# One block of exact products per batch: four projections moved behind a blockwise convolution

## The chip, the cores and the metric

The kernel runs on one core of a Trainium2 chip. The metric is device time in microseconds from one launch, the median over runs. Beside the runs there is one profiled execution, whose trace all views of the profile come from.

## What is computed

The input is `x` (32 batches of 512 rows by 512 columns, float32) and one 0/1 adjacency matrix of 512 by 512. Two layers follow each other:

```
# layer 0: attention over the graph, 8 heads of 64 columns, residual, layer norm
q, k, v = x @ Wq + bq, x @ Wk + bk, x @ Wv + bv
scores = einsum('bihd,bjhd->bhij', q, k) / 8 + where(adj == 0, -1e9, 0)
x = layernorm(x + einsum('bhij,bjhd->bihd', softmax(scores), v))
# layer 1: graph convolution, residual, layer norm
x = layernorm(x + (adj @ x) @ weight + bias)
```

## The kernel before, in words

**Exact products.** A product that must keep float32 accuracy is made of three passes on TensorE, each of four matmuls of 128x128 by 128x512. `split_high`, `split_rest` and `split_both` (L303 to L310) turn an operand into three factors, HIGH (by ACT), REST (by DVE) and BOTH (by POOL); the weights have such factors too. HIGH and REST passes add up in one PSUM bank, called near, the BOTH pass in another, called far. Everything that reads near and far adds them (`finish_projection`, L431, with ACT and DVE; `add_near` and `add_far`, L562 and L566, with DVE). The factors of the current left operand lie in three tiles of 128 x 4 x 512 that `factors` (L327) hands out; they have one buffer each, so x of batch b+1, then y of batch b-1 (the aggregated rows), then x of batch b+2 take turns in it.

**PSUM.** All eight banks are one ring (`bank`, L200): a new bank is the one that was given out eight banks ago, and TensorE waits until that has been read.

**The order.** The order of all instructions is written out by hand in `iteration(b)` (L805); each engine, and the queue of SP that issues the DMAs, works off its own in that order. `run` (L728) emits a list of steps, `merge` (L795) puts the k-th list of other steps behind the k-th of a list. `AFTER` (L882) hands steps over to the next iteration. Iteration b does, on TensorE:

1. `attend(b, 0)` and `attend(b, 1)`: the exponentials of heads 0 to 3 times v (L632).
2. `scores(b, 1)`: keys times queries of heads 4 to 7 (L609). DVE adds the mask while it empties a bank (L611), ACT takes the exponential in place (L613), POOL adds the four tiles of a pair of heads up (`add_exponentials`, L624) and `fold_squares` (L654) transposes that sum on DVE and reduces it to the softmax's denominators. Both tiles of POOL's sums and the eight exponential tiles are rings as well.
3. The first four of the eight projections of batch b+1 (`project`, L438; weights stream in from DRAM in chunks, `fetch_chunk`, three ahead).
4. `attend(b, 2)`, `attend(b, 3)`, then `scores(b + 1, 0)`.
5. The last four projections, the four blocks of v of batch b+1 (`project_values`, L461), the aggregation of batch b-1 with the adjacency matrix (`aggregate`, L527) and its convolution with the second layer's weight (`convolve`, L572), one block of rows after the other (`FIRST_TWO` and `whole`).

Between these stand, for the other engines: `turn_out` (L636, DVE transposes the attention's output and SP writes it out), `fetch_rows` (L648, it comes back transposed), `scale_rows` and `add_rows` (L693 and L700, ACT and POOL), `pass_parts`, `fetch_parts` and `add_up` (L668, L673 and L680, the denominators), `statistics`, `square_root`, `invert_root` and `normalise` (L478 to L501, the layer norms), `load_squares` and `turn_squares` (L223 and L344, x of batch b+2), `add_bias` (L547) and `store` (L513). `square_root` and the exponential need different function tables in ACT, so ACT loads a table (ACT_TABLE_LOAD) at each change.

In the kernel before, x of batch b+2 is split into factors after the whole convolution of batch b-1; the first projections that read it come in the next iteration, after two attends and a score block.

Of the kernel before, what the change touches and what calls it, by code (L numbers as in the profile page):

```python
# [9 lines left out]
FR = mybir.dt.float32r  # L10
# [8 lines left out]
P = 128  # L19
# [159 lines left out]
HIGH, REST, BOTH = 0, 1, 2  # L179
# [3 lines left out]
def fast_kernel(ctx: ExitStack, tc, verdict, x, adj, Wq, bq, Wk, bk, Wv, bv, W1, b1, out):  # L183
    nc = tc.nc
    B, N, D = x.shape
    H = Wq.shape[1] // HD
    HP = H // 2
    NB = N // P
    DB = D // P
# [4 lines left out]
    work = ctx.enter_context(tc.tile_pool(name="work", bufs=2))  # L194
# [5 lines left out]
    def bank(*shape):  # L200

        return psum.tile([P, *shape], FP, name="bank", tag="bank", bufs=8)
# [85 lines left out]
    def load_adjacency_rows(c):  # L288
        IN["adj", c] = work.tile([P, N], FP, name="adj_rows", tag="turn", bufs=TURNS)
        nc.sync.dma_start(IN["adj", c], adj[c * P:(c + 1) * P, :])  # L290
# [30 lines left out]
    def shrunk(w):  # L321
# [2 lines left out]
        nc.scalar.activation(temp, w, AF.Copy, scale=SHRINK)  # L324
        return temp

    def factors():  # L327
        return [work.tile([P, DB, N], FR, name=f"factors{f}", bufs=1) for f in (HIGH, REST, BOTH)]

    def x_transpose(c):  # L330

# [30 lines left out]
    def turns(b):  # L362
        return [(turn_squares, b, d) for d in range(DB)] if b < B else []
# [57 lines left out]
    def one_pass(f, pm, left, right, blocks=range(DB)):  # L421

        for d in blocks:
            nc.tensor.matmul(pm, left(f, d), right(f, d), start=(f != REST and d == 0),  # L424
                             stop=(f != HIGH and d == DB - 1))
# [43 lines left out]
    def projections(b):  # L469

        return [(project, b, which, m) for which, m in SEQUENCE] if b < B else []
# [90 lines left out]
    def add_near(b, r, near):  # L562
        row = X[b][:, r, :]
        nc.vector.scalar_tensor_tensor(row, near, 1.0 + EPSILON, row, op0=ALU.mult, op1=ALU.add)  # L564

    def add_far(b, r, far):  # L566
        row = X[b][:, r, :]
        nc.vector.tensor_add(row, far, row)  # L568

    NEAR, FAR = {}, {}  # L570

    def convolve(b, passes):  # L572

        yt = YT[b]
        for r, f, blocks in passes:
            if (b, r) not in NEAR:
                NEAR[b, r], FAR[b, r] = bank(N), bank(N)
            one_pass(f, (FAR if f == BOTH else NEAR)[b, r], lambda f, d: yt[f][:, d, r * P:(r + 1) * P],
                     lambda f, d: w1[:, f, d, :], blocks)
# [17 lines left out]
    E, ES, OUT, AT, ROWS, PART, INVERSE, TURNED, PASSED = ({} for _ in range(9))  # L597
# [28 lines left out]
    def attend(b, hp):  # L626
        po = bank(N)
        for j in range(NB):
            e = E.pop((b, hp, j))
            for s in range(2):  # L630
                h = 2 * hp + s
                nc.tensor.matmul(po[s * HD:(s + 1) * HD, :], V[b, j][:, h * HD:(h + 1) * HD], e[:, s, :],  # L632
                                 start=(j == 0), stop=(j == NB - 1))
        OUT[b, hp] = po

    def turn_out(b, hp):  # L636

        po = OUT.pop((b, hp))
        at = AT[b, hp] = work.tile([P, N], FP, name="attT")
        if b == B - 1:  # L640
            nc.scalar.activation(at, po, AF.Copy)  # L641
            return

        nc.vector.transpose(at, po)  # L644
        TURNED[b, hp] = passing.tile([P, N], FP, name="turned")
        nc.sync.dma_start(TURNED[b, hp], at)
# [69 lines left out]
    seen = consts.tile([P, 3], FP, name="seen")  # L716
# [11 lines left out]
    def run(units):  # L728
        for unit in units:
            unit[0](*unit[1:])  # L730
# [42 lines left out]
    def norm(t, which):  # L773

        if t - which < 0:
            return []
        lo, hi = which * NB, (which + 1) * NB
        return [(square_root, t, slice(lo, hi)), (invert_root, t, slice(lo, hi))] + [
            (normalise, t, slot) for slot in range(lo, hi)]

    def folds(b, g):
        return [(fold_squares, b, hp) for hp in range(g * PAIRS, (g + 1) * PAIRS)]

    def survey(b, which=1):
# [20 lines left out]
    def iteration(b):  # L805

        units = projections(b + 1)
        scaled, added = residuals(b, 0)
        later_scaled, later_added = residuals(b, 1)
        turned, divided = turns(b + 2), splits_of_x(b + 2)  # L810
        splits, gathered = aggregation(b - 1)
        squares = [(load_squares, b + 2, d) for d in range(DB)]
        folded = folds(b, 1)

        attend(b, 0)
        turn_out(b, 0)
        sooner, later = AFTER.pop(b - 1, ([], []))
        run(sooner)
        attend(b, 1)
        turn_out(b, 1)  # L820
        if b > 0:
            fetch_parts(b, 0)
        take_scores(b, 1)
        run(later)
        waiting = [(fetch_rows, b, 0), (fetch_rows, b, 1)]
        looking = 2 <= b < 2 + NB
        look = [(look_for_low_half, b - 2)] if looking else []
        ready = 1 if looking else 0 if b < 2 else 2
        run(waiting[:ready])
        if b == 0:  # L830
            run(merge(units[:4], [waiting + [(fold_squares, b, 1), (pass_parts, b, 0), (fetch_parts, b, 0)], [],
                                  [(add_up, b, 0)],
                                  folded[:1]]))
        else:
            old, young = norm(b - 1, 1), norm(b - 1, 0)
            roots = slice(0, 2 * NB if b > 1 else NB)
            if b == 1:
                run(survey(0, 0))
            run(merge(units[:4], [waiting[ready:]
                                  + [(square_root, b - 1, roots), (add_up, b, 0), (invert_root, b - 1, roots)],  # L840
                                  folded[:1] + old[2:], [(store, b - 2)] if b > 1 else [], young[2:] + scaled]))
        attend(b, 2)
        turn_out(b, 2)
        load(b)
        if looking:
            load_adjacency_rows(b - 2)
        attend(b, 3)
        turn_out(b, 3)
        if b == 0:
            run(scaled)  # L850
        later = scores(b + 1, 0)
        run(added + later + folded[1:])

        run(merge(units[4:], [[(pass_parts, b, 1), (fetch_parts, b, 1)], look, [(fold_squares, b + 1, 0)], splits[:2]]))
        units = values(b + 1)
        chunks = [(fetch_chunk, (b + 2) * len(SEQUENCE) + n) for n in range(AHEAD)]
        squares += [(fetch_rows, b, 2), (fetch_rows, b, 3), (pass_parts, b + 1, 0)] + chunks
        run(merge(units, [[(add_up, b, 1)], [(fold_squares, b + 1, 1)] + squares, later_scaled if b == B - 2 else [],
                          turned[:1] + (later_added if b == B - 2 else [])]))
        if b == B - 2:  # L860
            load(B - 1)
        if b == 0:
            split_last_weight()
        run(merge(gathered, [[unit] for unit in turned[1:]]))
        fresh, seen, shift = survey(b, 0), survey(b - 1), biases(b - 1)
        high, rest, both = divided
        if b == 0:
            run(high + rest + both[::-1] + later_scaled + later_added)
            return
        convolve(b - 1, FIRST_TWO)  # L870
        if b == B - 2:
            run([(add_row, b - 1, 0), (add_row, b - 1, 1)] + shift[:2] + fresh + seen[:2])
            return
        run(later_scaled + later_added[:1] + [(add_row, b - 1, 0)] + shift[:1] + later_added[1:])
        run([(add_row, b - 1, 1)] + shift[1:2] + seen[:1])
        convolve(b - 1, whole(2))
        run([(add_row, b - 1, 2)] + shift[2:3] + fresh[:1])
        convolve(b - 1, whole(3))
        run(high + rest + [(add_row, b - 1, 3)] + shift[3:] + both)
        AFTER[b] = (fresh[1:] + seen[1:2], seen[2:])  # L880

    AFTER = {}  # L882

# [80 lines left out]
    high, rest, both = splits_of_x(1)  # L964
# [73 lines left out]
```

## Time and profile before

| what | us |
|---|---|
| median of 3 runs (lowest to highest) | 2567.88 (2567.47 to 2568.14) |
| the profiled execution's own time | 2570.15 |
| its span, from first to last instruction | 2568.3 |
| PE busy | 2558.8 |
| DVE busy | 2058.3 |
| POOL busy | 1751.8 |
| ACT busy | 1528.5 |

The granted TensorE clock is 0.999 over the span. PE is TensorE's matmuls, PEld its weight loads, DVE the vector engine, ACT the scalar engine, POOL GpSimd, SP the engine whose queue issues the DMAs. In the timeline a line begins with its start and its length in us, then the engine, the source line, the operation, the tiles (written <- read), the shapes and how many instructions are merged in it; brackets tell idle time of the engine just before and what ended it. In the groups a line has busy time and the mean ns of one, then the idle time. A matmul of the attention in float32 shows as two records.

### The profile page before, as it was taken

How to read it: one execution, taken by the hardware profiler on the slowest of the kernel's cores; microseconds unless marked ns; L12 is line 12 of the kernel's file. 1: busy time of each engine (PE TensorE's matmuls, PEld its weight loads, DVE VectorE, ACT ScalarE, POOL GpSimd, SP SyncE). 2: the span in 40 equal slices, each digit the busy share in tenths (PEclk: the TensorE clock that was granted, in tenths of full speed). 3: DMA queues.
4: the chain of work that ended last, by engine and by line, in shares of the span. 5: the costliest groups of instructions: out<-in, count | busy, mean ns of one | idle time of the engine just before them, and what ended most of it. 6: DMA issues, size and time to landing. Idle time of an engine off the chain costs nothing.

```text
span 2568.3 us, 36882 instructions
## 1 busy us (share of the span) xinstructions
PE 2558.8 (100%) x11324; PEld 1692.3 (66%) x11324; DVE 2058.3 (80%) x3796; ACT 1528.5 (60%) x2540; POOL 1751.8 (68%) x1104
## 2 busy tenths in 40 slices
PE   9999999999999999999999999999999999999998
PEld 6676666666676666766667676666766667666666
DVE  8878878788787887877888778877787787887878
ACT  5656655666555666556665565655657556565555
POOL 4776667666676666766767676676766766666767
PEclk9999999999999999999999999999999999999999
DMA  9655554554545645456455465554655546555441
GB/s 266 167 158 150 161 154 117 165 156 151 166 113 150 168 138 163 125 138 177 136 156 133 133 174 138 164 133 123 173 143 160 148 113 167 146 158 163 108 121 52
DMA packets 747291, 380.59 MB, mean 148 GB/s; under 512 B 594896, under 2 KB 599248, under 8 KB 747088
## 3 DMA queue, kind: packets, MB, share of 16 engines
q1 hardware_dynamic: 746656, 377.51, 53.6%
q8 instruction: 93, 1.52, 0.3%
q14 instruction: 110, 0.90, 0.1%
q10 hardware_dynamic: 432, 0.66, 0.1%
HBM read 303.57 MB, written 74.45 MB: 147 GB/s over the span
## 4 chain that ended last, share of the span: by engine, by line
PE 99%; DVE 0%; DMA 0%; ACT 0%; issue 0%; DVEq 0%
PE bank L424 55%; PE bank L609 18%; PE bank L632 17%; PE bank L533 9%; PE bank L557 0%; DMA xin<-in_x_dram 0%; DVE bnst L484 0%; DVE xlast L564 0%; DVE xlast L568 0%; PE bank L336 0%; PE bank L708 0%; DVE shift L495 0%; PE bank L738 0%; ACT attT L641 0%; ACT xlast L1011 0%
## 5 line engine op out<-in xcount | busy, mean ns | idle before, releaser
L613 ACT ACTIVATE e<-e 128x1024 f32<-128x1024 f32 x512 | 525.7, 1055 | 309.0 <-DVE e L611 269.7
L424 PE MATMUL bank<-factors,stream 128*128 128x512 f32 x3012 | 703.2, 392 | 0.0
L424 PEld LDWEIGHTS bank<-factors,stream 128*128 128x128 f32 x3012 | 560.5, 188 | 163.4 <-DVE e L611 23.5
L624 POOL TENSOR_TENSOR es<-es,e 128x1024 f32<-128x1024 f32 x256 | 616.2, 2407 | 20.1
L611 DVE SCALAR_TENSOR_TENSOR e<-gap,bank 128x512 f32<-128x512 uint8 x1024 | 617.7, 678 | 12.5 <-PE bank L609 12.5
L624 POOL TENSOR_TENSOR es<-e 128x1024 f32<-128x1024 f32 x128 | 306.4, 2394 | 425.8 <-ACT e L613 423.4
L609 PE MATMUL bank<-q,k 64*128 64x512 f32 x2048 | 462.7, 598 | 0.0
L632 PE MATMUL bank<-e,v 128*64 128x512 f32 x2048 | 453.6, 595 | 0.0
L609 PEld LDWEIGHTS bank<-q,k 64*128 64x128 f32 x2048 | 203.2, 186 | 258.0 <-issue 159.0
L424 PE MATMUL bank<-w,factors 128*128 128x512 f32 x1536 | 354.3, 389 | 0.0
L424 PE MATMUL bank<-wv,factors 128*128 128x512 f32 x1536 | 353.5, 389 | 0.0
L698 ACT ACTIVATE rows<-rows,zero,inverse 128x64 f32<-128x64 f32 x992 | 335.1, 429 | 8.5 <-DVE inverse L685 8.5
L310 POOL TENSOR_TENSOR factors<-factors,factors 128x512 fp32r<-128x512 f32 x254 | 321.3, 1290 | 25.0 <-DVE factors L307 25.0
L424 PEld LDWEIGHTS bank<-wv,factors 128*128 128x128 f32 x1536 | 288.2, 188 | 60.6 <-DVE e L611 0.8
L424 PEld LDWEIGHTS bank<-w,factors 128*128 128x128 f32 x1536 | 288.0, 188 | 60.7 <-POOL factors L310 0.4
L632 PEld LDWEIGHTS bank<-e,v 128*64 128x64 f32 x2048 | 141.4, 137 | 278.4 <-issue 264.4
L510 ACT ACTIVATE high<-xs 128x512 fp32r<-128x512 f32 x124 | 74.4, 627 | 333.5 <-PE bank L533 333.4
L511 POOL TENSOR_TENSOR low<-xs,high 128x512 fp32r<-128x512 f32 x124 | 159.3, 1296 | 155.7 <-PE bank L533 155.7
L548 POOL TENSOR_TENSOR xs<-xs,b_r 128x512 f32<-128x512 f32 x124 | 160.3, 1294 | 125.7 <-DVE xs L568 125.7
L644 DVE STREAM_TRANSPOSE attT<-bank 128x512 f32<-128x512 f32 x124 | 87.8, 708 | 155.7 <-PE bank L632 152.8
L500 ACT ACTIVATE xs<-xs,shift,rstd 128x512 f32<-128x512 f32 x248 | 181.5, 805 | 14.8 <-DVE shift L495 14.8
L702 POOL TENSOR_TENSOR xs<-xs,rows 128x512 f32<-128x512 f32 x124 | 160.7, 1307 | 22.4 <-DMA stream<-kept_q 10.2
(98 smaller groups left out, 2431.4 us busy)
## 6 DMA issues: line engine op xcount, KB each, us to landing
stream<-kept_q SPq DMA_DIRECT2D x372, 256.0 KB, 4.7
stream<-kept_k SPq DMA_DIRECT2D x372, 256.0 KB, 3.6
xin<-in_x_dram SPq DMA_DIRECT2D x496, 64.0 KB, 2.3
turned<-attT SPq DMA_DIRECT2D x124, 256.0 KB, 3.3
rows<-turned SPq DMA_DIRECT2D x496, 64.0 KB, 2.5
xs<-in_x_dram SPq DMA_DIRECT2D x31, 1024.0 KB, 5.9
out_dram<-xs SPq DMA_DIRECT2D x31, 1024.0 KB, 5.2
part<-passed SPq DMA_DIRECT2D x256, 8.0 KB, 1.7
```

What stands on the lines that cost most here:

```text
L310: engine.tensor_sub(both, plain(high), plain(rest))
L424: nc.tensor.matmul(pm, left(f, d), right(f, d), start=(f != REST and d == 0), stop=(f != HIGH and d == DB - 1))
L500: nc.scalar.activation(row, row, AF.Identity, bias=SHIFT[t][:, slot:slot + 1], scale=RSTD[t][:, slot:slot + 1])
L533: nc.tensor.matmul(pm, part, adjT[:, n % NB, :], start=(n == 0), stop=(n == 2 * NB - 1))
L548: nc.gpsimd.tensor_add(X[b][:, c, :], X[b][:, c, :], b1_r)
L609: nc.tensor.matmul(ps[s], keys[:, j * P:(j + 1) * P], queries, start=True, stop=True)
L611: nc.vector.scalar_tensor_tensor(e[:, s, :], gap[:, j, :], NEG * root, ps[s], op0=ALU.mult, op1=ALU.add)
L613: nc.scalar.activation(e, e, AF.Exp, scale=1.0 / root)
L624: nc.gpsimd.tensor_add(ES[b, hp], ES[b, hp] if j > 1 else E[b, hp, 0], E[b, hp, j])
L632: nc.tensor.matmul(po[s * HD:(s + 1) * HD, :], V[b, j][:, h * HD:(h + 1) * HD], e[:, s, :], start=(j == 0), stop=(j == NB - 1))
L698: nc.scalar.activation(part, part, AF.Identity, bias=zero, scale=inverse[:, c, s:s + 1])
L702: nc.gpsimd.tensor_add(cols, cols, ROWS.pop((b, hp)))
```

## The change

For 2 <= b <= 30 the first four projections of batch b+1 are no longer in the middle of the attention. They were made at the end of the iteration before, behind the convolution. For that, the convolution takes all eight banks at once (`open_banks`) and goes block by block through the contraction (`block(d)`: for each of HIGH, REST, BOTH one matmul for each of the four row blocks), so that block d of the factors is read for the last time early and block d of x of batch b+2 is split behind it. `factors` gives out one lasting set of tiles instead of a new one each time. The steps of other engines that were merged with those four projections have new places: the square root and its inversion, with `add_up(b, 0)`, behind `attend(b, 0)`; the older normalisations and the store between the two first attends; `fold_squares(b, 2)` ahead of `attend(b, 3)`; `scale_rows` ahead of `scores(b + 1, 0)`; the younger normalisations behind the first of the last four projections. The three chunks for the moved projections are fetched ahead of the loads of squares, and `fetch_parts(b + 1, 0)` follows `pass_parts` at once.

```
+    shared = [work.tile([P, DB, N], FR, name=f"factors{f}", bufs=1) for f in (HIGH, REST, BOTH)]
     def factors():
-        return [work.tile([P, DB, N], FR, name=f"factors{f}", bufs=1) for f in (HIGH, REST, BOTH)]
+        return shared
...
+    def open_banks(b):
+        for table in (NEAR, FAR):
+            for r in range(NB):
+                table[b, r] = bank(N)
+
+    def block(d):
+        return [(r, f, range(d, d + 1)) for f in (HIGH, REST, BOTH) for r in range(NB)]
...
+        old, young = norm(b - 1, 1), norm(b - 1, 0)
...
         attend(b, 0)
+        if b > 1:
+            roots = slice(0, 2 * NB)
+            run(sooner + [(square_root, b - 1, roots), (add_up, b, 0), (invert_root, b - 1, roots)])
         turn_out(b, 0)
-        run(sooner)
+        run(old[2:] + [(store, b - 2)] if b > 1 else sooner)
         attend(b, 1)
         turn_out(b, 1)
-        if b > 0:
+        if (b, 0) in PASSED:
             fetch_parts(b, 0)
         take_scores(b, 1)
         run(later)
...
         else:
-            run(merge(units[:4], [waiting[ready:]
-                                  + [(square_root, b - 1, roots), (add_up, b, 0), (invert_root, b - 1, roots)],
-                                  folded[:1] + old[2:], [(store, b - 2)] if b > 1 else [], young[2:] + scaled]))
+            run(waiting)
         attend(b, 2)
         turn_out(b, 2)
         load(b)
...
+        if b > 1:
+            run(folded[:1])
         attend(b, 3)
         turn_out(b, 3)
-        if b == 0:
+        if b != 1:
             run(scaled)
         later = scores(b + 1, 0)
-        run(added + later + folded[1:])
-        run(merge(units[4:], [[(pass_parts, b, 1), (fetch_parts, b, 1)], look, [(fold_squares, b + 1, 0)], splits[:2]]))
+        run(added + later + folded[b > 0:])
+        run(merge(units[4:], [[(pass_parts, b, 1), (fetch_parts, b, 1)] + (young[2:] if b > 1 else []), look, [(fold_squares, b + 1, 0)], splits[:2]]))
...
-        squares += [(fetch_rows, b, 2), (fetch_rows, b, 3), (pass_parts, b + 1, 0)] + chunks
+        if 0 < b < B - 2:
+            run(chunks)
+            squares += [(fetch_rows, b, 2), (fetch_rows, b, 3), (pass_parts, b + 1, 0), (fetch_parts, b + 1, 0)]
...
-        run(later_scaled + later_added[:1] + [(add_row, b - 1, 0)] + shift[:1] + later_added[1:])
-        run([(add_row, b - 1, 1)] + shift[1:2] + seen[:1])
-        convolve(b - 1, whole(2))
-        run([(add_row, b - 1, 2)] + shift[2:3] + fresh[:1])
-        convolve(b - 1, whole(3))
-        run(high + rest + [(add_row, b - 1, 3)] + shift[3:] + both)
-        AFTER[b] = (fresh[1:] + seen[1:2], seen[2:])
+        open_banks(b - 1)
+        run(later_scaled[:1] + later_added[:1])
+        for d in range(DB - 1):
+            convolve(b - 1, block(d))
+            run(high[d:d + 1] + rest[d:d + 1] + both[d:d + 1])
+        convolve(b - 1, block(DB - 1))
+        run(high[DB - 1:])
+        for r in range(NB):
+            add_near(b - 1, r, NEAR.pop((b - 1, r)))
+            if r == NB // 2 - 1:
+                run(rest[DB - 1:] + both[DB - 1:])
+        run(later_scaled[1:] + later_added[1:])
+        for r in range(NB):
+            add_far(b - 1, r, FAR.pop((b - 1, r)))
+            run(shift[r:r + 1])
+        run(merge(projections(b + 2)[:4], [[], fresh[:2], fresh[2:], seen[:2]]))
+        AFTER[b] = (seen[2:], [])
```

More of the change, by code (lines that the diff above doesn't have):

```diff
@@ L813, in iteration @@
         folded = folds(b, 1)
+        old, young = norm(b - 1, 1), norm(b - 1, 0)
+        waiting = [(fetch_rows, b, 0), (fetch_rows, b, 1)]
+        looking = 2 <= b < 2 + NB
+        look = [(look_for_low_half, b - 2)] if looking else []
+        sooner, later = AFTER.pop(b - 1, ([], []))
         attend(b, 0)
+        if b > 1:
+            roots = slice(0, 2 * NB)
+            run(sooner + [(square_root, b - 1, roots), (add_up, b, 0), (invert_root, b - 1, roots)])
         turn_out(b, 0)
-        sooner, later = AFTER.pop(b - 1, ([], []))
-        run(sooner)
+        run(old[2:] + [(store, b - 2)] if b > 1 else sooner)
         attend(b, 1)
         turn_out(b, 1)
-        if b > 0:
+        if (b, 0) in PASSED:
             fetch_parts(b, 0)
@@ L824, in iteration @@
         run(later)
[L825 to L829, printed above, removed]
-        if b == 0:
-            run(merge(units[:4], [waiting + [(fold_squares, b, 1), (pass_parts, b, 0), (fetch_parts, b, 0)], [],
-                                  [(add_up, b, 0)],
-                                  folded[:1]]))
-        else:
[L835 to L838, printed above, removed]
-            run(merge(units[:4], [waiting[ready:]
-                                  + [(square_root, b - 1, roots), (add_up, b, 0), (invert_root, b - 1, roots)],
-                                  folded[:1] + old[2:], [(store, b - 2)] if b > 1 else [], young[2:] + scaled]))
+        if b == 0:
+            run(merge(units[:4], [waiting + [(fold_squares, b, 1), (pass_parts, b, 0), (fetch_parts, b, 0)], [], [],
+                                  [(add_up, b, 0)]]))
+        elif b == 1:
+            roots = slice(0, NB)
+            run(survey(0, 0))
+            run(merge(units[:4], [waiting + [(square_root, b - 1, roots), (add_up, b, 0), (invert_root, b - 1, roots)],
+                                  folded[:1], [], young[2:] + scaled]))
+        else:
+            run(waiting)
         attend(b, 2)
@@ L846, in iteration @@
             load_adjacency_rows(b - 2)
+        if b > 1:
+            run(folded[:1])
         attend(b, 3)
         turn_out(b, 3)
-        if b == 0:
+        if b != 1:
             run(scaled)
         later = scores(b + 1, 0)
-        run(added + later + folded[1:])
-        run(merge(units[4:], [[(pass_parts, b, 1), (fetch_parts, b, 1)], look, [(fold_squares, b + 1, 0)], splits[:2]]))
+        run(added + later + folded[b > 0:])
+        run(merge(units[4:], [[(pass_parts, b, 1), (fetch_parts, b, 1)] + (young[2:] if b > 1 else []), look, [(fold_squares, b + 1, 0)], splits[:2]]))
         units = values(b + 1)
         chunks = [(fetch_chunk, (b + 2) * len(SEQUENCE) + n) for n in range(AHEAD)]
-        squares += [(fetch_rows, b, 2), (fetch_rows, b, 3), (pass_parts, b + 1, 0)] + chunks
+        if 0 < b < B - 2:
+            run(chunks)
+            squares += [(fetch_rows, b, 2), (fetch_rows, b, 3), (pass_parts, b + 1, 0), (fetch_parts, b + 1, 0)]
+        else:
+            squares += [(fetch_rows, b, 2), (fetch_rows, b, 3), (pass_parts, b + 1, 0)] + chunks
         run(merge(units, [[(add_up, b, 1)], [(fold_squares, b + 1, 1)] + squares, later_scaled if b == B - 2 else [],
@@ L869, in iteration @@
             return
-        convolve(b - 1, FIRST_TWO)
         if b == B - 2:
+            convolve(b - 1, FIRST_TWO)
             run([(add_row, b - 1, 0), (add_row, b - 1, 1)] + shift[:2] + fresh + seen[:2])
             return
-        run(later_scaled + later_added[:1] + [(add_row, b - 1, 0)] + shift[:1] + later_added[1:])
-        run([(add_row, b - 1, 1)] + shift[1:2] + seen[:1])
-        convolve(b - 1, whole(2))
-        run([(add_row, b - 1, 2)] + shift[2:3] + fresh[:1])
-        convolve(b - 1, whole(3))
-        run(high + rest + [(add_row, b - 1, 3)] + shift[3:] + both)
-        AFTER[b] = (fresh[1:] + seen[1:2], seen[2:])
+        open_banks(b - 1)
[15 more added lines that the diff above has]
+        AFTER[b] = (seen[2:], [])
     AFTER = {}
```

## The prediction, made before the changed kernel was run

> **What bounds the kernel now.** I read the page first: busy shares, then the chain that ended last.
>
> ```profile
> PE 2558.8 (100%) x11324; PEld 1692.3 (66%) x11324; DVE 2058.3 (80%) x3796; ACT 1528.5 (60%) x2540; POOL 1751.8 (68%) x1104
> ...
> PE 99%; DVE 0%; DMA 0%; ACT 0%; issue 0%; DVEq 0%
> ```
>
> TensorE is the whole chain, so only time between matmul starts can be won. A busy PE hides that; the timeline of PE alone, over one batch, shows it by the starts of its blocks.
>
> ```profile
> 1295.17 11.04 PE L424 MATMUL bank<-w,factors 128*128 128x512 f32 x48
> 1306.14 7.09 PE L632 MATMUL bank<-e,v 128*64 128x512 f32 x32
> 1313.16 7.21 PE L609 MATMUL bank<-q,k 64*128 64x512 f32 x32
> 1320.30 11.19 PE L424 MATMUL bank<-factors,stream 128*128 128x512 f32 x48
> 1331.42 7.09 PE L632 MATMUL bank<-e,v 128*64 128x512 f32 x32
> 1338.43 7.21 PE L609 MATMUL bank<-q,k 64*128 64x512 f32 x32
> 1345.57 11.22 PE L424 MATMUL bank<-factors,stream 128*128 128x512 f32 x48
> 1356.63 11.04 PE L424 MATMUL bank<-wv,factors 128*128 128x512 f32 x48
> ```
>
> Differences of starts are the prices. Convolution 10.97, attend 7.02, scores 7.14, first four projections 11.12, attend 7.01, scores 7.14, last four 11.06, values 10.88 (the next block, L533, starts at 1367.51), aggregation 7.25: 79.59 us a batch. Values is 48 exact matmuls with its own kind on both sides, 10.88/48 = 0.227 us each. So the convolution pays 0.09 for its exit to attention, the first projections 0.24 for entry and exit, the last four 0.18. Nothing else waits long.
>
> The second thing to read is how DVE, ACT and POOL follow a score block, since the change puts two score blocks close together. The timelines of those engines:
>
> ```profile
> 1314.32 9.65 DVE L611 SCALAR_TENSOR_TENSOR e<-gap,bank 128x512 f32<-128x512 uint8 x16
> ...
> 1327.53 1.06 DVE L495 TENSOR_SCALAR shift<-stat,rstd 128x1 f32<-128x1 f32 x8
> ...
> 1329.11 1.30 DVE L662 STREAM_TRANSPOSE square<-es 128x512 f32<-128x512 f32 x2
> 1330.32 1.24 DVE L664 TENSOR_REDUCE part<-square 128x16 f32<-128x512 f32 x2
> ```
>
> ```profile
> 1315.64 9.43 ACT L613 ACTIVATE e<-e 128x1024 f32<-128x1024 f32 x8 [8.95 <-DVE e L611]
> ...
> 1325.66 1.28 ACT L488 ACT_TABLE_LOAD   x1
> 1326.96 0.30 ACT L488 ACTIVATE rstd<-stat,eps 128x8 f32<-128x8 f32 x1
> ...
> 1328.32 2.94 ACT L500 ACTIVATE xs<-xs,shift,rstd 128x512 f32<-128x512 f32 x4 [0.49 <-DVE shift L495]
> ...
> 1340.96 1.28 ACT L613 ACT_TABLE_LOAD   x1 [0.43 <-DVE e L611]
> ```
>
> ```profile
> 1317.97 2.37 POOL L624 TENSOR_TENSOR es<-e 128x1024 f32<-128x1024 f32 x1 [2.33 <-ACT e L613]
> 1320.42 4.90 POOL L624 TENSOR_TENSOR es<-es,e 128x1024 f32<-128x1024 f32 x2
> ...
> 1344.33 2.39 POOL L624 TENSOR_TENSOR es<-e 128x1024 f32<-128x1024 f32 x1 [11.48 <-ACT e L613]
> ```
>
> DVE empties 16 score banks at a pitch of 0.60 us (9.65/16); PE fills them at 0.43. With 8 banks PE meets DVE at the last score pair: in the list of single matmuls it is held 0.08 us there. So **each tenth that DVE starts a score block late holds PE for a tenth**. POOL's first sum starts 4.81 us after the first scores (1317.97-1313.16) and its third ends at +12.16; in the second score block, where a table load stands before the exponential, the first starts at +5.90.
>
> **The skill.** "Perfetto Trace Analysis", Identifying the Most-Contended Engine, says matmul busy share is a poor measure because pipelined matmuls look busy; the trace agrees, 100% busy with 1.3 us a batch of seams. "TensorE: Matmul & The Clock Gate", Wait — 56ns, not 53.3ns?, gives 215.7 ns start to start at N=512; here it is 227, and I use 227. "ScalarE: Activation LUTs", What ACT_TABLE_LOAD costs, gives 1283 ns plus a 1.38 us drain for a change of set; the trace has the 1.28 us and no drain (the load starts 0.02 after the instruction before it). "PSUM — Partial Sum Buffer" has nothing I need beyond the 8 banks.
>
> **The change part by part.** It acts for b = 2 to 30, 29 batches; batches 0 and 1 keep their projections in attention, and I put their small shifts at 0.
>
> *PE's order.* The first four projections of batch b+2 follow the convolution, so one entry and one exit go. Convolution 10.97 becomes 10.88, first projections 11.12 become 10.97 (exit kept): 0.24 a batch. New is scores straight to attend. No trace row shows it; attend to scores costs about 0.14 (7.02 against 16 pairs at 0.43), the removed exit to projections about 0.10; bounds 0 to 0.20 for the new one, so the saving lies between 0.14 and 0.34. I take 0.10: 0.24 x 29 = 7.0 us.
>
> *Convolution by blocks.* The same 48 matmuls, 2.72 us a block. All 8 banks are taken at once; those of the aggregation are read 1.5 us after it ends, FAR row 3 is first written at +2.5. The split of x for block d (ACT 0.62, DVE 0.69, POOL 1.29) fits inside block d+1. For the last one: bank 0 is finished at +9.1, DVE adds rows 0 and 1, the rest is written by +11.4, POOL's difference by +12.8; the projection starts at 10.88 and reads that at +13.4. 0.6 us spare, cost nothing. Cover gone, it costs its overrun. The add_near and add_far pairs end near +15, before the third projection needs FAR's banks at +16.3. Rows scaled on ACT (8 x 0.33) and POOL's biases lie beside projections.
>
> *One lasting tile* removes only the release of the whole tile; 0 by itself.
>
> *SP's queue.* Nine chunk loads go ahead of 16 loads of squares, at 0.45 us an issue: squares come 4 us later, against some 4 spare before their transposes; the same loads are gone from behind. pass_parts and fetch_parts of b+1 stand last, as pass_parts does now. The store waits for four normalisations and holds turned's second issue by about 1 us; its rows are read 10 us later. Cost 0, bound 1 us a batch.
>
> *Steps moved into attention.* Queued behind the last projection now: its add, four statistics (0.61 and 3.25 us), square root (table load already done; 0.35), then 1.06 to the first normalisation (inversion and shifts), four of them 2.94, Exp's table load 1.30. Counting from the first attend matmul, the add starts at +0.11, so the load ends at 0.11+0.61+3.25+0.35+1.06+2.94+1.30 = +9.62, which is 2.60 after the first score matmul S (7.02). The second exponential starts at S+3.68 where nothing is in its way (1316.84), and ACT, at its pitch of 0.95 back to back, is ready for it at S+3.55: **0.1 spare**. DVE itself is free for the first scores about 0.7 us early.
>
> *fold_squares before attend(b, 3).* DVE waits here for POOL's third sum, and turn_out 3 and all 16 scores of the next batch are queued behind it. POOL S+12.16, plus two transposes and two reductions 2.38 and 0.04 latency = S+14.58, turn_out 0.66, first score read S+15.24. PE reaches the second scores at S+7.14+7.01 = S+14.15, and DVE can start 1.17 later (1339.60-1338.43), S+15.32. **On time by 0.08.** Cost 0, between 0 and 1 us. A gain is excluded: DVE can't start ahead of PE.
>
> *Scaling rows ahead of the second exponentials* ends at about S+17.3 against S+16.7: exponentials 0.6 late, but a table load of 1.28 is gone there, so POOL is no later than now. young's normalisations and splits keep over 4 us before the aggregation.
>
> **Sum.** -7.0 us. Against the profiled execution (span 2568.3, 2570.15 with what lies around it) 2563.1; that execution is 2.3 above the median of the runs, so 2567.9-7.0 = 2560.9, say 2561.
>
> **The rivals.**
> - *Slower: Exp's table load waits for the first scores.* At 1340.96 it waits for DVE, and all 30 such loads do; the Sqrt load doesn't. If it waits in its new place, POOL starts at +5.90 instead of +4.81, the fold and the scores behind it are 1.09-0.08 = 1.01 late: 29 x (1.01-0.24) = +22, 2590. It decides from a slip of 0.24. Against: there the exponential waits on POOL too, which ACT has seen by then in the new place. Chance 0.13.
> - *Nothing: the same loop slips by 0.06 to 0.4* through links of 0.05 each that I took from other places; 29 x 0.2 eats 6 of the 7 us: 2567. For it speaks that two spares are 0.1. Chance 0.21.
> - *It doesn't do what it says: the tile is guarded as a whole*, so the splits of x start only after the convolution and the projection waits 1.5 us or more: 29 x (1.5-0.24) = +37, 2604. Against: the convolution starts at 1374.76 while the last splits of y, from 1375.59 on, are still being written to the same tile. Chance 0.04.
>
> **Numbers.** Forecast 0.62, its own range 2558 to 2564 (0.14 to 0.34 a batch). The first rival's smaller slips and the second one reach to 2576. The interval 2556 to 2576 leaves out most of the 0.17 of the slow cases. Within 0.2% (5.1 us, about what a measurement of this kernel can tell from no change): faster 0.60, same 0.23, slower 0.17.
>
> **What would show it.** Right: one block of 96 exact matmuls of L424 in 21.8 us, no gap at its middle, 29 fewer entries, attend after scores in 7.0, the second score block 7.14 long. Wrong: a second score block of 7.5 or more with DVE idle before L662 until POOL; a load of Exp that waits for DVE; a seam between convolution and projections; DVE's transposes of x waiting for DMA.

## The result and the profile after

| | before | after |
|---|---|---|
| median of 16 runs each, us | 2567.78 | 2572.60 |
| lowest to highest, us | 2567.47 to 2568.81 | 2570.34 to 2576.92 |
| the profiled execution's own time, its span, us | 2570.15, 2568.3 | 2576.02, 2574.2 |

The ratio is 1.002, with a 95% interval of 1.0013 to 1.0028. The forecast was 2561: the sign is wrong. The spread is new as well: 6.6 us between the runs of the changed kernel, 1.3 before. That suggests that something in it depends on when transfers land; experiment two tests this.

The page of the changed kernel, busy shares and chain:

```profile
PE 2558.8 (99%) x11324; PEld 1698.1 (66%) x11324; DVE 2095.9 (81%) x3796; ACT 1549.8 (60%) x2540; POOL 1764.6 (69%) x1104
...
PE 95%; DVE 2%; POOL 1%; issue 1%; DMA 0%; ACT 0%; SPq 0%; POOLq 0%; DVEq 0%; ACTq 0%
```

PE is 95% of the chain and no longer 99%: DVE and POOL now end waits of PE. In most batches the order of PE looks as predicted. Its timeline over one batch:

```profile
1301.68 11.04 PE L426 MATMUL bank<-w,factors 128*128 128x512 f32 x48
1312.56 11.09 PE L426 MATMUL bank<-factors,stream 128*128 128x512 f32 x48
1323.58 7.09 PE L642 MATMUL bank<-e,v 128*64 128x512 f32 x32
1330.60 7.21 PE L619 MATMUL bank<-q,k 64*128 64x512 f32 x32
1337.74 7.09 PE L642 MATMUL bank<-e,v 128*64 128x512 f32 x32
1344.76 7.28 PE L619 MATMUL bank<-q,k 64*128 64x512 f32 x32
1351.96 11.17 PE L426 MATMUL bank<-factors,stream 128*128 128x512 f32 x48
1362.98 11.04 PE L426 MATMUL bank<-wv,factors 128*128 128x512 f32 x48
```

By differences of starts: convolution 10.88, first projections 11.02 (10.97 in most batches), attend 7.02, scores 7.14, attend 7.02, second scores 7.20, last projections 11.02. From one convolution to the next it is 79.38 to 79.45 us where nothing else happens; before, it was 79.59 on average. So **the gain is there, 0.2 us a batch**, and two losses sit on top of it.

**Loss one, once: batches 0 and 1.** PE's timeline there:

```profile
111.79 1.94 PE L642 MATMUL bank<-e,v 128*64 128x512 f32 x8
115.95 1.08 PE L642 MATMUL bank<-e,v 128*64 128x512 f32 x4 [2.23 <-DVE v L469]
117.35 4.51 PE L642 MATMUL bank<-e,v 128*64 128x512 f32 x20 [0.31 <-DVE v L469]
121.79 2.85 PE L619 MATMUL bank<-q,k 64*128 64x512 f32 x12
125.00 6.48 PE L619 MATMUL bank<-q,k 64*128 64x512 f32 x20 [0.36 <-DVE attT L654]
```

The attend takes 10.00 us (121.79-111.79) in place of 7.02, and the scores 9.61 (to 131.40) in place of 7.14: 5.45 us. PE waits for v, which DVE writes. DVE's timeline shows why it is late, and POOL's shows what DVE itself waited for:

```profile
112.04 1.31 DVE L672 STREAM_TRANSPOSE square<-es 128x512 f32<-128x512 f32 x2 [3.55 <-POOL es L634]
113.27 1.24 DVE L674 TENSOR_REDUCE part<-square 128x16 f32<-128x512 f32 x2
114.42 0.68 DVE L468 SCALAR_TENSOR_TENSOR v<-bank,bv_r 128x512 f32<-128x512 f32 x1
115.21 0.69 DVE L469 TENSOR_TENSOR v<-bank,v 128x512 f32<-128x512 f32 x1
```

```profile
94.82 2.41 POOL L634 TENSOR_TENSOR es<-e 128x1024 f32<-128x1024 f32 x1 [14.59 <-DVE square L672]
```

POOL stood still for 14.59 us until DVE had transposed an older sum. In the kernel before, the same sum starts at 87.87. The sums have two buffers. In batch 0 the changed order puts `fold_squares(0, 2)` behind the scores of batch 1 (`folded[b > 0:]` is the whole list there), so DVE empties the buffer only after all 16 masks, POOL starts 7 us late, and DVE's later fold, queued ahead of v, waits for POOL.

**Loss two, in some batches: a seam between the convolution and the projections behind it.** The largest is in the batch whose convolution starts at 504.0: convolution 11.47, projections 12.35, 1.97 us too much. The chain of waits there:

```profile
504.17 8.17 PE bank L426 x36
512.35 0.04 issue
512.39 1.82 DVE factors L307 x2
514.21 0.49 issue
514.70 0.74 DVE xs L566 x2
515.44 0.46 issue
515.89 1.84 DVE factors L307
...
517.90 1.27 POOL factors L310
519.17 0.04 issue
519.21 0.97 PE bank L426 x3
```

PE is done with its blocks and waits for the split of x: REST on DVE, `add_near`, the last REST, then BOTH on POOL, which ends at 519.17, 15.2 us after the convolution's start; the prediction had 12.8, needed at 13.4. (From here on, +15.2 means 15.2 us after the start of the batch's convolution.) It is late because ACT started the split late: ahead of it stands `scale_rows` of heads 4 and 5, which began only at 507.79, at +3.8 in place of +0.7. It waits for rows to come back from DRAM. SP's timeline shows the queue, first of the changed kernel:

```profile
490.81 11.49 SPq L232 DMA_DIRECT2D xin<-in_x_dram  x16
502.40 6.12 SPq L662 DMA_DIRECT2D rows<-turned  x8
```

Then of the kernel before, in the same batch, whose convolution starts at 499.15:

```profile
483.67 4.15 SPq L232 DMA_DIRECT2D xin<-in_x_dram  x8
487.92 5.32 SPq L652 DMA_DIRECT2D rows<-turned  x8
```

The issue of these rows begins 11.2 us ahead of the convolution before, 1.6 us ahead of it after. Nine chunk loads now stand in front, 4.0 us of issue (three of them take 1.28 to 1.33); and the 16 loads of squares behind them took 0.72 us each (11.49/16), against 0.52 before (4.15/8). In eight batches, whose rows are scaled 2.1 us or more after the convolution's start, the seam is open by 0.35 us or more; where it is 1.8 or less, projections take 10.97 to 11.03. In the profiled execution the eight cost 6 us together, and it ran 3.4 us longer than the median.

How lateness becomes a seam shows best where it is small. In the batch whose convolution starts at 1619.83, rows are scaled at +2.1 and the seam is 0.35. DVE's timeline there, with the last REST:

```profile
1630.53 1.35 DVE L307 SCALAR_TENSOR_TENSOR factors<-factors,turn 128x512 fp32r<-128x512 f32 x1
```

POOL's, with the third and the last BOTH:

```profile
1630.04 1.29 POOL L310 TENSOR_TENSOR factors<-factors,factors 128x512 fp32r<-128x512 f32 x1
1632.02 1.30 POOL L310 TENSOR_TENSOR factors<-factors,factors 128x512 fp32r<-128x512 f32 x1 [0.69 <-DVE factors L307]
```

DVE's again, one batch earlier (convolution at 1540.38), where no seam opens:

```profile
1551.08 0.68 DVE L307 SCALAR_TENSOR_TENSOR factors<-factors,turn 128x512 fp32r<-128x512 f32 x1
```

The last REST starts at +10.70 in both batches. With late rows POOL's third BOTH is still under way at that moment, and the REST takes 1.35 and not 0.68. In six of the eight batches the last BOTH ends later than the usual +12.8 by just what this REST is stretched (0.67 to 1.11 us). In the other two, at 504.0 and 585.4, REST or BOTH is stretched as well. So the late rows reach the seam by pushing POOL's part of the split into DVE's.

### The profile page after: what moved, and what is told of

Same layout as the page of the kernel before. It is cut to its first block, busy times and chain, and to the rows that moved or that the text cites. A ratio compares the mean times of both kernels' runs of the same rounds, so it can differ in the third digit from the quotient of the medians.

```text
span 2574.2 us, 37273 instructions
## 1 busy us (share of the span) xinstructions
PE 2558.8 (99%) x11324; PEld 1698.1 (66%) x11324; DVE 2095.9 (81%) x3796; ACT 1549.8 (60%) x2540; POOL 1764.6 (69%) x1104
## 4 chain that ended last, share of the span: by engine, by line
PE 95%; DVE 2%; POOL 1%; issue 1%; DMA 0%; ACT 0%; SPq 0%; POOLq 0%; DVEq 0%; ACTq 0%
PE bank L426 52%; PE bank L619 18%; PE bank L642 17%; PE bank L535 9%; DVE factors L307 1%; POOL es L634 0%; POOL factors L310 0%; DVE e L621 0%; PE bank L559 0%; DMA rows<-turned 0%; ACT rows L708 0%; DVE xs L566 0%; DMA xin<-in_x_dram 0%; DVE bnst L486 0%; SPq L662 0%
## 5 line engine op out<-in xcount | busy, mean ns | idle before, releaser
L623 ACT ACTIVATE e<-e 128x1024 f32<-128x1024 f32 x512 | 534.1, 1056 | 60.3 <-DVE e L621 11.3
L310 POOL TENSOR_TENSOR factors<-factors,factors 128x512 fp32r<-128x512 f32 x254 | 341.4, 1358 | 82.2 <-DVE factors L307 55.7
L307 DVE SCALAR_TENSOR_TENSOR factors<-factors,turn 128x512 fp32r<-128x512 f32 x124 | 134.0, 1106 | 119.9 <-ACT factors L304 88.7
L672 DVE STREAM_TRANSPOSE square<-es 128x512 f32<-128x512 f32 x256 | 166.1, 687 | 24.6 <-POOL es L634 24.6
```

The costliest lines, as they stand in the source:

```text
L307: nc.vector.scalar_tensor_tensor(rest, plain(high), -1.0 / EPSILON, a, op0=ALU.mult, op1=ALU.add)
L310: engine.tensor_sub(both, plain(high), plain(rest))
L623: nc.scalar.activation(e, e, AF.Exp, scale=1.0 / root)
L672: nc.vector.transpose(squares[s], es[:, s, :])
```

## The experiments

The gain of about 6, the loss of 5.45 and the loss of some 4 to 6 were the theory from the traces. The rivals were that something else than the rows opens the seam (the length of the split itself, DVE against POOL), and that the score loop of the prediction's first rival had slipped. All times are medians; ratios are to the kernel before. "The first kernel", "the third kernel" are those of experiments one and three.

**One: batch 0's fold back behind its fourth projection.**

```diff
-                                  [(add_up, b, 0)]]))
+                                  [(add_up, b, 0)] + folded[:1]]))
...
-        run(added + later + folded[b > 0:])
+        run(added + later + folded[1:])
```

> Only batch 0 is changed back: its fold_squares(0, 2) stands behind its fourth projection again and no longer behind the scores of batch 1. Theory A (one-off): in the changed kernel POOL's first sum of batch 1 waits 14.6 us for that fold, and TensorE pays for it in the first attend and score block of batch 1 (10.00 and 9.61 instead of 7.02 and 7.14), 5.45 us once. Then this run is about 5 us below the changed kernel: 2567.5, and both blocks have their usual lengths. Rival (the loss is spread over all batches by the score loop): less than 1 us changes.

2569.18 us (2567.10 to 2572.97), ratio 1.0007 (0.9998 to 1.0015). The two blocks are back at 7.02 and 7.14. Of the 5.45 us only 3.4 show in the medians, and the spread of 5.9 stays: the seams are still open, in other batches (five by 0.70 to 2.1 us each, three by 0.13 to 0.26).

**Two: the chunk loads back behind the squares and the rows in SP's queue.**

```diff
-            run(chunks)
-            squares += [(fetch_rows, b, 2), (fetch_rows, b, 3), (pass_parts, b + 1, 0), (fetch_parts, b + 1, 0)]
+            squares += [(fetch_rows, b, 2), (fetch_rows, b, 3), (pass_parts, b + 1, 0), (fetch_parts, b + 1, 0)] + chunks
```

> The nine chunk loads go back behind the loads of squares and of rows in SP's queue; all else as in the changed kernel. Theory B: rows of heads 4 and 5 land 1.6 us after the convolution's start because of them (6.5 us before it in the kernel before), ACT waits for them ahead of the splits of x, and the last split is late at the seam; the projections' block then is up to 1.4 us longer, 5 to 6 us in all in the profile. Then the rows land before the convolution starts, all seams close (21.8 us for the 96 matmuls in every batch), the run is 3 to 5 us below the changed kernel, 2568.5, and repeats within 1 us instead of 6.6. Rival (the collisions of DVE and POOL are enough by themselves): the seams stay as long.

2569.24 us (2568.82 to 2569.64), ratio 1.0005 (0.9997 to 1.0014). Every seam is closed (10.88 and 10.97 in each batch), rows are scaled at +0.7 in each, and the spread falls from 6.6 to 0.8. SP's timeline of this kernel, in the batch whose convolution starts at 503.2, has the squares at 0.53 us an issue again and the rows 9.9 us ahead:

```profile
484.76 8.43 SPq L232 DMA_DIRECT2D xin<-in_x_dram  x16
493.29 5.33 SPq L662 DMA_DIRECT2D rows<-turned  x8
```

The stall of batches 0 and 1 (5.6 us) is still in it. So the order in SP's queue makes the second loss and the spread.

**Three: both edits together.**

> Both edits together. If theories A and B are independent the gains add up: 2572.6 - 5 - 4 = 2563.5, 0.17% below the kernel before, which is what the removed entries are worth in the trace (79.59 - 79.41 = 0.18 us a batch, 5 us in all). If something else holds the kernel back it stays near 2568.

2563.65 us (2562.82 to 2564.01), ratio **0.9983 (0.9977 to 0.9990): faster than both kernels**. Both losses are undone and the rest of the change stays. Each edit alone gained 3.4 us on the changed kernel, both together 9.0. So in the medians the losses don't simply add up: the seams cost 3.4 us beside the stall and 5.5 without it. Why is open. Its profiled execution took 2563.05, span 2561.3, where the forecast from the profile was 2563.1 before it was shifted to the medians. PE's share of the chain is back:

```profile
PE 99%; DVE 0%; ACT 0%; issue 0%; DVEq 0%
```

**Four: chunks early, but the rows of heads 4 and 5 scaled and added behind the last block of the convolution.** This leaves SP's queue as the change has it and takes the rows away from ahead of the split.

```diff
-        run(later_scaled[:1] + later_added[:1])
...
-        run(later_scaled[1:] + later_added[1:])
+        run(later_scaled + later_added)
```

> Chunk loads stay early; instead scaling and adding of rows of heads 4 and 5 move behind the convolution's last block, to those of heads 6 and 7. Theory B: the late rows then stand in nobody's way; the first DVE and POOL splits begin with the first block, the seams close, 3 to 5 us below the changed kernel, 2568.5. If the seams come from collisions of DVE's and POOL's splits with each other, they stay and the time with them.

2569.68 us (2569.06 to 2570.08), ratio 1.0007 (0.9999 to 1.0015). The seams are closed in all batches, as in the second experiment, and the stall at the start stays. So what the late rows cost, they cost by standing ahead of the split. The edit moves ACT's scaling and POOL's adding of the rows together, so it doesn't tell the two apart; in the trace above it is HIGH, on ACT, that starts late.

The kernels five to eight, and ten, start from the third.

**Five: only the transposes of `fold_squares(b, 2)` ahead of `attend(b, 3)`, its reductions behind the scores.** The second score block takes about 7.21 and not 7.14 in all kernels so far since the change; the prediction had put the fold in front of it with 0.08 to spare.

```diff
-            run(folded[:1])
+            run([(fold_squares, b, 2, True)])
...
-        run(added + later + folded[1:])
+        run(added + later + ([(reduce_squares, b, 2)] if b > 1 else []) + folded[1:])
```

> On top of the kernel with both edits: of fold_squares(b, 2) ahead of attend(b, 3) only the two transposes stay, the two reductions (1.2 us) go behind the scores of batch b+1. The prediction had DVE ready for the second score block 0.08 us ahead of TensorE; with both edits it starts 0.06 late (S+15.39) and that block takes 7.21 instead of 7.14. If that is the fold's length, DVE is now 1.1 us early, the block takes 7.14, and 29 x 0.07 = 2 us go: 2561.6. If something else holds the block, the time stays at 2563.6.

2563.39 us (2563.01 to 2563.92), ratio 0.9982 (0.9974 to 0.9989): no gain, and the block still takes 7.21, though DVE now stands idle for 0.37 us ahead of its first mask, where it was 0.17. The fold isn't what holds it. In the trace, DVE's first mask has a second wait in the changed order, on ACT, right ahead of it, and starts 1.23 us after PE's first score instead of 1.17. That this wait is the cause is argued, not shown.

**Six: the four younger normalisations ahead of the first exponentials** (2.9 us more on ACT there), to see whether the loop is as tight as predicted.

```diff
-        run(old[2:] + [(store, b - 2)] if b > 1 else sooner)
+        run(young[2:] + old[2:] + [(store, b - 2)] if b > 1 else sooner)
```

> On top of both edits: the four younger normalisations stand with the older ones ahead of the first exponential, 2.86 us more of ACT there. If the loop of the prediction (normalisations, table load, second exponential, POOL's three sums, fold, turn_out, scores) has no slack, the second exponential is 2.74 late, so are POOL's third sum and the second score block, which takes about 9.8 instead of 7.2: 29 x 2.6 = 75, about 2639. If there is slack that the arithmetic missed, less than half of that.

2622.5 us, one run. The second score block of PE, and DVE ahead of it:

```profile
1281.37 9.33 PE L619 MATMUL bank<-q,k 64*128 64x512 f32 x32
```

```profile
1281.68 1.30 DVE L672 STREAM_TRANSPOSE square<-es 128x512 f32<-128x512 f32 x2 [2.90 <-POOL es L634]
```

The block takes 9.26 us (to 1290.63), 2.05 more than 7.21, and DVE idles 2.90 us until POOL's sum. 2.05 x 29 = 59, and the run is 58.9 above the third kernel. ACT's first exponential is 2.33 us late and not the 2.74 expected, since the younger normalisations start 0.49 earlier than the older ones did. Of the 2.33, 2.05 reach PE: the loop has 0.3 us of slack.

**Seven: the convolution by rows again, the projections behind it.**

```diff
+        convolve(b - 1, FIRST_TWO + whole(2) + whole(3))
         for d in range(DB - 1):
-            convolve(b - 1, block(d))
```

> On top of both edits: the convolution goes row block by row block as in the kernel before, with the projections behind it. If going through the contraction is what lets the projections follow without a gap, POOL now makes its four differences behind the convolution's end, the last at about +5.7, where the projection reads it at +2.5: the 96 matmuls take 3.2 us longer in each of 28 batches, +90, about 2654. If the lasting tile alone were enough, no gap.

2677.23 us, one run. In the batch shown, convolution 13.23 and projections 12.34, 3.7 us more; on average a batch takes 3.9 us more. PE's timeline:

```profile
1262.65 11.04 PE L426 MATMUL bank<-w,factors 128*128 128x512 f32 x48
1275.88 1.86 PE L426 MATMUL bank<-factors,stream 128*128 128x512 f32 x7 [2.19 <-issue]
1278.17 1.20 PE L426 MATMUL bank<-factors,stream 128*128 128x512 f32 x4 [0.43 <-DVE factors L307]
1279.61 8.68 PE L426 MATMUL bank<-factors,stream 128*128 128x512 f32 x37 [0.25 <-POOL factors L310]
```

Without the blocks REST starts at +9.6 (1272.21) and not at +4.0, and PE waits for the last BOTH until +17.0 (1279.61). The blocks are worth about 114 us.

**Eight: `fold_squares(b, 2)` behind the scores in all batches from 2 on,** as batch 0 has it in the changed kernel.

```diff
-        if b > 1:
-            run(folded[:1])
...
-        run(added + later + folded[1:])
+        run(added + later + folded[b < 2:])
```

> On top of both edits: in all batches from 2 on, fold_squares(b, 2) stands behind the scores of batch b+1, as the change has it in batch 0 alone. DVE is then on time for the scores, but POOL's first sum of batch b+1 waits for the fold, 7 us more than now. In batch 0 that cost 5.45 us, where POOL also splits the last weight. In the other batches POOL has some 5 us to spare before its part of the aggregation: about 1 us a batch, 2580, if the harm goes by POOL's lateness; 29 x 5.4 = 157, about 2720, if it goes by the wait itself.

2676.26 us, one run. The stall lies elsewhere than in batch 0: the aggregation takes 10.47 us in place of 7.25. PE's timeline:

```profile
1254.63 1.19 PE L535 MATMUL bank<-adjT,low 128*128 128x512 f32 x4 [0.54 <-POOL low L513]
...
1262.44 1.21 PE L535 MATMUL bank<-adjT,low 128*128 128x512 f32 x4 [2.08 <-POOL low L513]
```

POOL's first sum waits 7.11 us for the fold in this batch, as expected; its later work moves with it, and `low` is behind the sums in its queue. In eleven batches the convolution takes 1.4 to 1.7 us more too, which is not taken apart here. Together it is 3.2 to 5 us a batch, 3.9 on average, between the two forecasts. The fold has to stand ahead of `attend(b, 3)` to free POOL's buffer in time.

**Nine and ten: BOTH of x made by DVE instead of POOL,** on the first kernel and on the third. If POOL at the end of the split were the cause of the seam, this should close it without any change in SP's queue.

```diff
-        split_both(*(XT[b][f][:, d, :] for f in (BOTH, HIGH, REST)))
+        split_both(*(XT[b][f][:, d, :] for f in (BOTH, HIGH, REST)), nc.vector)
```

> On top of the batch-0 edit alone, so with the chunk loads early and the rows late: the BOTH factors of x are made by DVE (0.68) and not by POOL (1.29), so that DVE's REST and POOL's BOTH can't collide. In the changed kernel REST of x takes 1.11 us in the mean instead of 0.69 and BOTH up to 1.75 instead of 1.29. If these collisions are what turns late rows into gaps, moderate lateness (rows scaled at +2 to +2.5) no longer opens a seam, the last split is done at about +12.1, and the run is 3 to 4 us below the batch-0 edit alone, 2566, with a smaller spread. If the late rows alone do it, the seams stay and so does 2569.

2575.19 us (2571.89 to 2576.97), ratio 1.0022 (1.0012 to 1.0032): 6.4 us above the kernel before as run beside it, where the first kernel was 1.3 above. The seam is open again where rows are late: with rows at +3.8 the convolution takes 12.76 and the projections 11.58. With rows at +2.6 to +2.7 it is 1.7 us wide, against 0.7 to 0.8 in the first kernel.

> The same on top of both edits. Seams are closed there already, with 0.6 us to spare, so nothing should move: 2563.6, within 0.5, with REST of x near 0.7 us but where the added rows still meet it. If DVE's 2.4 us more a batch delay the statistics behind the last projection, the second score block grows above 7.2 and the time with it.

2567.49 us (2566.78 to 2568.00), ratio 0.9994 (0.9986 to 1.0003). Both missed. The reason is at the start again, where x's split stands ahead of DVE's last transpose before a score block. DVE's timeline in the tenth kernel:

```profile
56.94 2.50 DVE L310 TENSOR_TENSOR factors<-factors,factors 128x512 fp32r<-128x512 f32 x4
59.36 0.71 DVE L654 STREAM_TRANSPOSE attT<-bank 128x512 f32<-128x512 f32 x1
59.99 7.22 DVE L621 SCALAR_TENSOR_TENSOR e<-gap,bank 128x512 f32<-128x512 uint8 x12
```

That score block takes 8.80, a later one 9.48, in place of 7.14: 4.0 us once, in both kernels. Measured from the kernel before as run beside each, the ninth lies 5.0 us above the first and the tenth 2.9 above the third. All later batches of the tenth are 79.37 to 79.42 us apart, as in the third. So POOL as the maker of BOTH isn't needed for a seam: with late rows it opens without that, and with rows in time it stays shut with it. That collisions of DVE and POOL play no part is not shown. In the four widest seams of the ninth kernel a step of the split on DVE is stretched too, now beside POOL's adding of the rows of heads 6 and 7: the last BOTH takes 1.59 to 1.73 in three of them in place of 0.69, the last REST 1.34 in the fourth. Late rows without any collision were not run.

**Eleven: the kernel before once more, profiled,** since between profiles the third kernel gained 7.1 us and between medians 4.2.

> A second profiled execution of the kernel before, nothing changed. The first one took 2570.15 us where the median of the runs is 2567.8, and its score block at 82.00 was 1.00 us too long while its batches were a steady 79.60 us apart. If that block and the start of the launch are what varies, this one has batches of 79.60 us again and comes out at 2567.5 to 2568.5 with the block back at about 7.14 us. If the batches vary, they come out at about 79.52 us (2.3 us over 29 batches) and the gain per batch of the changed kernel is about 0.13 and not 0.21 us.

2570.02 us, beside an unprofiled run of 2569.06. Its batches are 79.59 us apart on average (79.53 to 79.61), and the score block at 82.26 again takes 8.04. Neither expectation held: the two profiles of before agree, and both lie 2.2 to 2.4 us above the 2567.8 of its runs (0.96 above the one run beside the second), while that of the third kernel lies 0.6 below its own. Why is open.

## Why the prediction was wrong

Its sum had one gain and a row of zeros. The gain was right in kind and somewhat too large, and two of the zeros were wrong.

- **PE's order, -7.0: right in place, a little too large.** Convolution 10.88, projections 10.97, scores to attend 7.14 as taken. Last projections give 0.04 that wasn't counted, the second score block takes back 0.07 that wasn't either. From one convolution to the next the third kernel needs 79.39 against 79.60, 0.21 in place of 0.24: 29 x 0.21 = 6.1 in the trace. The rest of its 7.0 between spans is a score block at 82, 1.0 us shorter than before; that the spans differ by just the forecast 7.0 is luck. The medians differ by 4.2 only.
- **"Batches 0 and 1 keep their projections in attention, and I put their small shifts at 0": wrong, +5.45.** The diff shows that the fold of batch 0 goes behind the scores, and it was the kind of step the prediction costed for the other batches. What it needed was the question who waits for the buffer that this fold empties: POOL, 14.59 us.
- **"SP's queue ... Cost 0, bound 1 us a batch": wrong, about 6 in the profile, 3.4 between the medians of the changed and the second kernel, 5.5 between those of the first and the third.** The 4 us of chunk issues were counted, and compared with the slack of the squares' transposes. But the loads behind the squares were not followed. In the batch shown, rows moved from 11.2 us ahead of the convolution to 1.6 ahead, 9.6 later: 4.4 by the chunks with the gaps between them, 3.0 by squares issued more slowly, 2.2 because the fetch of parts ahead of them all came later there. In the median of the batches they moved from 10.8 ahead to 3.6. And the step that waits for them, `scale_rows` of heads 4 and 5, stands in ACT's order ahead of the split.
- **"0.6 us spare, cost nothing": right where rows are in time, but the spare is about 0.3.** Rows at +0.7, the last BOTH ends at +12.8, as worked out, and no seam opens. The projections need it by about +13.1 and not +13.4: where it ends at +12.87 there is no seam, at +13.12 one of 0.04, at +13.49 one of 0.35. The spare is eaten from rows at about +2 on. One term was mis-sized: REST of x at 0.69. With rows in time that does no harm; with late rows the stretched last REST is what the six batches above pay for. The groups of L307, before in the first fence and after in the second:

```profile
L307 DVE SCALAR_TENSOR_TENSOR factors<-factors,turn 128x512 fp32r<-128x512 f32 x124 | 78.8, 692 | 11.2 <-PE bank L424 10.5 <-ACT factors L304 0.7
```

```profile
L307 DVE SCALAR_TENSOR_TENSOR factors<-factors,turn 128x512 fp32r<-128x512 f32 x124 | 134.0, 1106 | 119.9 <-ACT factors L304 88.7
```

692 ns became 1106. The Trainium skill explains it in "SBUF — State Buffer", SBUF: two separate sides: a DVE operation with two SBUF inputs and a GpSimd operation that reads SBUF want the same pair of ports; the one that starts first has them for the whole instruction, and the other is blocked. The trace agrees: in the third kernel REST takes 0.68 us in the median alone and 1.36 where a POOL operation is under way as it starts; one that starts at +4.0 ends at +5.4, 0.6 after the POOL operation that ran from +3.5 to +4.8.
- **The score loop, "on time by 0.08": right.** Exp's load runs without waiting, so the first rival is out. ACT's timeline in the changed kernel:

```profile
1329.09 2.93 ACT L502 ACTIVATE xs<-xs,shift,rstd 128x512 f32<-128x512 f32 x4 [1.10 <-DVE shift L497]
1332.03 1.28 ACT L623 ACT_TABLE_LOAD   x1
1333.33 9.18 ACT L623 ACTIVATE e<-e 128x1024 f32<-128x1024 f32 x8
```

With S the start of the first score block (1330.60), the load starts at S+1.43, 0.01 after the normalisations, and POOL's first sum starts at S+4.81, the very number of before. The fold began at S+12.13, predicted 12.20.
- **The rivals.** The second, "the same loop slips", has a slip of the size at its lower edge (0.07 us, x 29 = 2) but not its cause: the fifth experiment shows that it isn't the fold. The third, a tile guarded as a whole, is out: splits were under way in the convolution. None of the three was what happened.

## What to carry to other kernels

When loads are moved ahead in a queue, follow every load behind them to the step that waits for it, and then what is queued behind that step on its own engine; here the victim was two groups of loads further on and blocked a third thing. Late work also meets other work than it used to: look at what then runs beside it on the other engine. When a step that empties a ring's buffer is moved, ask who fills it next, above all in the first batches, where the order is a different one. Here a spread between runs that grew from 1.3 to 6.6 us came from a wait for a transfer on the path; with the chunks back in place it was 0.8.

## What the runs showed of the hardware

- Issues of 64 KB loads on SP took 0.72 us each behind nine loads of 256 KB, against 0.52 to 0.53 without them just ahead (11.49/16 and 8.43/16). As a mean over the 16 loads of a batch it is 0.66 to 0.78 in the changed kernel and 0.52 to 0.61 in the second.
- An Exp table load whose exponential's data is there starts 0.01 us after the instruction ahead of it, and the exponential 0.02 after the load's end (1332.03+1.28 to 1333.33).
- One REST of 0.69 us on DVE takes 1.36 when it meets a POOL operation of 1.30 us that also reads SBUF; in the tenth kernel, with BOTH on DVE, its mean falls from 1010 to 845 ns.
